# The output product of a two-layer graph kernel: from a two by two by two to a two by three by three scheme

## The chip, the cores and the metric

The kernel runs on one core of one Trainium2 chip. The metric is the device time of one execution in microseconds; before the change it is 2888.91 us, the median of three runs (2888.81 to 2894.07).

## What is computed

Two layers over 128 graphs of 64 nodes with 768 features, all in float32. Cut to what matters:

```python
def _L1_gnn_ref(seq_inputs, Wq, bq, Wk, bk, Wv, bv, Wf, bf, graph_mask):
    q = _heads(seq_inputs @ Wq + bq)          # 6 heads of 128
    k = _heads(seq_inputs @ Wk + bk)
    v = _heads(seq_inputs @ Wv + bv)
    scores = jnp.einsum('bhqd,bhkd->bhqk', q, k) / np.sqrt(HEAD_SIZE)
    probs = jax.nn.softmax(scores + bias, axis=-1)
    ctx = jnp.einsum('bhqk,bhkd->bhqd', probs, v)
    ctx = ctx.transpose(0, 2, 1, 3).reshape(...)
    return ctx @ Wf + bf

x = _layernorm(x + _L0_gnn_ref(x, adj, ...))  # tanh attention of 12 heads, elu, gate
x = _layernorm(x + _L1_gnn_ref(x, ..., adj))
```

The change concerns the last product, `ctx @ Wf + bf`, with the residual `x +` around it.

## The kernel before

The 8192 rows (tokens) are 64 tiles of 128 rows; two tiles make a pair, four a quad. Phase A runs over the 32 pairs and computes layer 0 and layer 1's values v; phase B runs over the 16 quads and computes queries, keys, attention and the output. Every large product of 768 by 768 is made by a scheme of seven products instead of eight (`TURNS`): tokens, inner features and output features are each split in two, seven sums of blocks of the tokens meet seven sums of blocks of the matrix, and the seven results are added up in a certain way. A weight matrix therefore lies in SBUF as seven blocks of 384 by 384 (`places`). The sums for the first layer's matrices are made in place; those of wq, wk and wf are made on GpSimd during phase A by `to_there`, which loads small pieces into a free part of `zone`, sums them and stores seven blocks to DRAM, and `matrix` loads them back later.

The order of the work on each engine is written out. A class `Beat` keeps a clock whose unit is one product: `beat.product` emits the matmuls of one product and puts the read of its result 1.5 beats later; `beat.start` steps a generator whose yields are waits in beats; `tick` emits what has become due. This fixes the order in which instructions stand in each engine's queue. The engines then run through their queues freely, waiting only on semaphores.

Phase B, for a quad q and f = 0, 1, 2 (each f is a pair of heads):

- `queries` and `keys` (both `by_feature`, matmuls on L417): seven products of three matmuls of 256 columns. Results stand in three PSUM sums. P1 is copied by ACT (L397) or biased (L400), P6 and P5 are read by VectorE into `q_u`/`k_u` (L393), P7 by L403, P3 by L409, P4 by L406. P7 and P4 stand in the same PSUM sum, so P4's matmuls wait for P7's read.
- `slab`: the attention of one f. Scores `s_ps` (L936), mask and maximum on VectorE (L946, L950), L952, the exponential on ACT, sum, reciprocal, L961, then a copy on ACT (L975), a transposing DMA (L976), two copies (L980), the product with v `c_ps` (L992), two copies (L1006), two transposing DMAs (L1007) and four copies into `cT` (L1014). Its steps stand beats apart and interleave with the products. For the very last f the transposes are made on TensorE (L970, L990).
- for the quad before, at f = 1 the first output (i = 0) and at f = 2 the second (i = 1), each of a pair of tiles: `operands` makes the four sums of tokens on VectorE (L290, tile `sc`, a single buffer) during `keys`; `rows_of` loads the pair's rows of layer 0 (`y`, L1034) and adds the bias on GpSimd (L1039); `output` follows the keys with `by_token` (L321): seven products of three matmuls of 384 columns in three PSUM sums. P1 is copied by ACT (L1058), VectorE reads the others (L1063 to L1082), GpSimd adds rows to three of the parts (L1052). `normed` then takes the statistics on VectorE, the power on GpSimd (L345, L346), scales on ACT (L1093) and stores the rows (L1095).

All DMAs stand in SP's queue, in the order in which they were emitted; a DMA that waits holds the ones behind it. PSUM has five buffers (`dense_b`) for sums in phase B. The bias of the values goes through wf into `bf_sb` once, by `last_bias` (L898), between queries and keys of q = 1, f = 0.

Of the kernel before, what the change touches and what calls it, by code (L numbers as in the profile page):

```python
# [27 lines left out]
F32 = mybir.dt.float32  # L31
# [3 lines left out]
ALU = mybir.AluOpType  # L35
# [4 lines left out]
P = 128  # L40
N = 64
D = 768
KC = D // P
KH = KC // 2
HALF = D // 2
H0, E0 = 12, 64
H1, E1 = 6, 128
BANK = 512
# [8 lines left out]
W11, W21, W22, T1, T2, T3, N4 = range(7)  # L57
# [13 lines left out]
    ("P4", 1, X22, N4),  # L71
)

# [53 lines left out]
class Beat:  # L127
# [31 lines left out]
    def tick(self):  # L159
        while self.events and self.events[0][0] < self.now + 1:  # L160
            heapq.heappop(self.events)[-1]()
        self.now += 1

    def until(self, there):
        while not there():
# [8 lines left out]
def two_layers(  # L174
# [21 lines left out]
    nc = tc.nc  # L196
# [19 lines left out]
    bv_sb = const.tile([P, KC], F32, name="bv_sb")  # L216
# [3 lines left out]

    places = [const.tile([P, 7, KH, HALF], F32, name=f"w_{i}") for i in range(3)]
    place = {"w0": 0, "h_w": 1, "wv": 2, "wq": 0, "wk": 1, "wf": 2}
# [18 lines left out]
        engine.tensor_tensor(t[:, N4], t[:, W21], t[:, T2], ALU.subtract)  # L241


    w_there = {n: dram.tile([P, 7, KH, HALF], F32, name=f"{n}_there") for n in ("wq", "wk", "wf")}

    def to_there(w, name):
        blocks = w.rearrange("(k c p) (m q n) -> k m c q p n", k=2, p=P, m=2, n=P)
# [49 lines left out]
    def sums_of_tokens(engine, s, b11, b12, b21, b22):  # L297

        if engine is nc.vector:
            plus(s[:, 0], b21, b22)  # L300
            plus(s[:, 1], s[:, 0], b11, ALU.subtract)
            yield 1
            plus(s[:, 2], b11, b21, ALU.subtract)
            plus(s[:, 3], b12, s[:, 1], ALU.subtract)
        else:
            engine.tensor_tensor(s[:, 0], b21, b22, ALU.add)
            engine.tensor_tensor(s[:, 1], s[:, 0], b11, ALU.subtract)
            yield 1
            engine.tensor_tensor(s[:, 2], b11, b21, ALU.subtract)
            engine.tensor_tensor(s[:, 3], b12, s[:, 1], ALU.subtract)  # L310

    def by_token(name, blocks, w, reads):

        sums = [sb(dense[0], [P, BANK], "dense", f"{name}{i}") for i in range(3)]
        begun = set()
        for what, to, xb, wb in TURNS:
            ps = sums[to][:, 0:HALF]

            def emit():
                for c in range(KH):  # L320
                    nc.tensor.matmul(  # L321
                        ps,
                        lhsT=blocks[xb][:, c, :],
                        rhs=w[:, wb, c, :],
                        start=(c == 0 and to not in begun),
                        stop=(c == KH - 1),
                        skip_group_check=True,
                    )
# [35 lines left out]
    ready, dense = {}, []  # L364
# [69 lines left out]
    def phase_a(pa, ps_a, dst_pool):  # L434
# [400 lines left out]
        for p in range(n_pairs):  # L835
            ta, tb = tiles_of(p)
            A = {"t": ta, "p": p, "side": 0}
# [38 lines left out]
    blocks = {}  # L876
# [9 lines left out]


    def phase_b(pb, ps_b):
        beat.start(matrix("wf", 1), 2)
        bf_sb = row(bf, "bf_sb", pb)  # L890

        def last_bias():

            for m, parts in enumerate((((0, W11), (1, W21)), ((0, W11), (0, T1), (1, W22)))):
                ps = sb(dense[0], [P, BANK], "dense", f"bias_ps_{m}")[:, 0:HALF]
                steps = [(k * KH + c, wb, c) for k, wb in parts for c in range(KH)]
                for i, (at, wb, c) in enumerate(steps):
                    nc.tensor.matmul(  # L898
                        ps,
                        lhsT=bv_sb[:, at : at + 1].to_broadcast([P, P]),  # L900
                        rhs=ready["wf_sb"][:, wb, c, :],
                        start=(i == 0),
                        stop=(i == len(steps) - 1),
                    )
                to = bf_sb[:, m * HALF : (m + 1) * HALF]
                nc.vector.tensor_tensor(to, to, ps, ALU.add)

        def part(name):
            return sb(pb, [P, HALF], "part", name, 7)

        def load(Q):

# [106 lines left out]
        def operands(Q, i):  # L1019

            while not Q.get("done"):
                yield 1
            q, c = Q["q"], Q["c"][i]
            s = sb(pb, [P, 4, KH, P], "sc", f"sc_{q}_{i}", 1)
            b = [c[:, 0, :, 0], c[:, 1, :, 0], c[:, 0, :, 1], c[:, 1, :, 1]]
            yield from sums_of_tokens(nc.vector, s, *b)
            Q["ob", i] = b + [s[:, k] for k in range(4)]

        def rows_of(Q, i):
            q = Q["q"]  # L1030
# [9 lines left out]
                yield 1  # L1040

        def output(Q, i):
            q = Q["q"]
            ya, yb = Q["y", i, 0], Q["y", i, 1]
            lo, hi = slice(0, HALF), slice(HALF, D)
            u = {}
            name = f"o_{q}_{i}_"

            def with_rows(k, of, y, m):
                def work():  # L1050
                    u[k] = part(f"{name}{k}")
                    nc.gpsimd.tensor_tensor(u[k], u[of], y[:, m], ALU.add)  # L1052

                beat.soon(work)

            def p1(ps):
                u[1] = part(f"{name}1")
                nc.scalar.copy(u[1], ps)  # L1058
                with_rows(4, 1, yb, lo)

            def p6(ps):
                u[2] = part(f"{name}2")
                nc.vector.tensor_tensor(u[2], u[1], ps, ALU.add)  # L1063
                with_rows(5, 2, ya, hi)

            def p2(ps):
                nc.vector.tensor_tensor(ya[:, lo], ya[:, lo], ps, ALU.add)

            def p5(ps):
                u[3] = part(f"{name}3")  # L1070
                nc.vector.tensor_tensor(u[3], u[1], ps, ALU.add)
                with_rows(6, 3, yb, hi)

            def p7(ps):
                nc.vector.tensor_tensor(yb[:, hi], u[6], ps, ALU.add)

            def p4(ps):
                nc.vector.tensor_tensor(yb[:, lo], u[4], ps, ALU.add)
                beat.start(normed(yb, 4 * q + 2 + i), 0)

            def p3(ps):
                nc.vector.tensor_tensor(ya[:, hi], u[5], ps, ALU.add)  # L1082
                beat.start(normed(ya, 4 * q + i), 0)

            by_token(name, Q["ob", i], ready["wf_sb"], dict(P1=p1, P2=p2, P3=p3, P4=p4, P5=p5, P6=p6, P7=p7))
# [18 lines left out]
        for q in range(n_quads + 1):  # L1104
            for f in range(3):
                if q < n_quads and (q or f):
                    queries(q, f, blocks, part)
                if q == 1 and f == 0:
                    last_bias()
# [72 lines left out]
```

## Time and profile before

The profiled execution took 2889.98 us, of which the span from first to last instruction is 2888.1; the granted clock of TensorE was 0.992 on average.

| | us |
|---|---|
| median of three runs | 2888.91 |
| profiled execution, its span | 2889.98, 2888.1 |
| phase A, up to the first queries of phase B | 1455.7 |
| TensorE busy from 1500 to 2800 us | 1300.0 of 1300 |
| VectorE busy from 2000 to 2500 us | 227 of 500 |
| GpSimd busy from 2000 to 2500 us | 96 of 500 |
| output product L321 (`o`), 1344 records | 471.3 |
| bias product L898, 30 records | 9.8 |
| GpSimd's row additions L1039, 64 of 1.81 | 114.8 |
| GpSimd's additions L1052, 96 of 1.12 | 107.3 |

How to read it: PE is TensorE, PEld its weight loads, DVE is VectorE, POOL is GpSimd, SPq is SP issuing DMAs. A group such as `o<-w,sc` is named by what it writes and reads. Busy time of PE overlaps: a record of 256 columns lasts 0.38 us in the table, but the next one starts 0.22 later.

### The profile page before, as it was taken

The page shows a single profiled execution, that of the slowest core. Times are in us where ns is not written, and L with a number is a line of the kernel's source. Part 1 is how long each engine was busy: PE and PEld are TensorE (multiplying, and loading weights), DVE is VectorE, ACT ScalarE, POOL GpSimd, SP SyncE. Part 2 cuts the span into 40 slices and gives each one's busy share as a digit, 9 for nine tenths or more (in the row PEclk, how much of TensorE's full clock was granted, in tenths as well). Part 3 has the DMA queues.
Part 4 walks back from the last instruction along what each step waited for, and adds up shares of the span by engine and source line. Part 5 has one row for each costly group of instructions (what it writes and reads, how often), then busy time and mean ns, then how long its engine had stood idle before and what let it go on. Part 6 is the DMA issues. An engine that isn't in the chain of part 4 may idle for free.

```text
span 2888.1 us, 42411 instructions
## 1 busy us (share of the span) xinstructions
PE 2825.2 (98%) x15586; PEld 1927.7 (67%) x15586; DVE 1851.1 (64%) x3555; ACT 1324.3 (46%) x1594; POOL 1182.0 (41%) x1106
## 2 busy tenths in 40 slices
PE   7899999999999999999799999999999999999998
PEld 4455555555555555555577777777777787877775
DVE  6887888888888988888534444444444444444444
ACT  2655555655556655665423333333333343333332
POOL 5666767767666656665201111221212211112113
PEclk9999999999999999999899999999999999999999
DMA  6677777778776666667864354443544434544432
GB/s 203 152 181 210 192 189 210 197 193 206 187 195 170 177 166 175 177 164 200 231 172 109 95 121 118 110 121 81 123 120 124 103 99 106 130 123 103 110 94 79
DMA packets 670350, 434.29 MB, mean 150 GB/s; under 512 B 442816, under 2 KB 616384, under 8 KB 670144
## 3 DMA queue, kind: packets, MB, share of 16 engines
q1 hardware_dynamic: 670144, 431.59, 58.0%
q8 instruction: 123, 2.02, 0.3%
q14 instruction: 83, 0.68, 0.1%
HBM read 199.07 MB, written 132.32 MB: 115 GB/s over the span
## 4 chain that ended last, share of the span: by engine, by line
PE 90%; DVE 3%; DMA 3%; ACT 1%; issue 0%; SPq 0%; POOL 0%; POOLq 0%; DVEq 0%; ACTq 0%
PE o L321 15%; PE k L417 15%; PE q L417 15%; PE v L321 14%; PE h L321 13%; PE g L321 12%; PE f_all L723 2%; PE s_ps L936 2%; PE c_ps L992 2%; DMA th_d<-bc_e 1%; ACT bc_e L714 0%; PE bias_ps L898 0%; DMA elu_turned<-xg_parts 0%; DVE mix L748 0%; DVE mix L753 0%
## 5 line engine op out<-in xcount | busy, mean ns | idle before, releaser
L321 PE MATMUL h<-w,zone 128*128 128x384 f32 x1320 | 448.4, 495 | 22.6 <-ACT h L514 12.4
L417 PE MATMUL q<-zone,w 128*128 128x256 f32 x2016 | 452.1, 382 | 6.9 <-issue 4.0
L417 PE MATMUL k<-zone,w 128*128 128x256 f32 x2016 | 446.2, 381 | 0.9 <-ACT k_u L397 0.9
L321 PE MATMUL g<-w,zone 128*128 128x384 f32 x1320 | 442.2, 490 | 4.8 <-DVE gate L568 3.7
L417 PEld LDWEIGHTS q<-zone,w 128*128 128x128 f32 x2016 | 382.5, 191 | 68.6 <-issue 6.2
L417 PEld LDWEIGHTS k<-zone,w 128*128 128x128 f32 x2016 | 380.6, 190 | 57.0 <-issue 5.0
L1039 POOL TENSOR_TENSOR y<-y,bf_sb 128x768 f32<-128x768 f32 x64 | 114.8, 1813 | 741.7 <-DMA y<-x_there 638.5
L321 PEld LDWEIGHTS h<-w,zone 128*128 128x128 f32 x1320 | 250.9, 192 | 196.5 <-ACT h L514 13.6
L321 PEld LDWEIGHTS g<-w,zone 128*128 128x128 f32 x1320 | 248.2, 190 | 177.5 <-DVE gate L568 12.7
L321 PE MATMUL o<-w,sc 128*128 128x384 f32 x768 | 268.0, 493 | 2.8 <-DVE sc L290 2.8
L345 POOL TENSOR_TENSOR rs<-rs,power 128x1 f32<-128x1 f32 x128 | 71.1, 556 | 460.6 <-DVE rs L343 460.6
L321 PE MATMUL v<-w,x_sums 128*128 128x384 f32 x768 | 258.5, 486 | 0.9 <-DVE x_sums L290 0.9
L643 POOL TENSOR_TENSOR bc_e<-th_d,w_dst_sb 128x768 f32<-128x768 f32 x64 | 119.8, 1873 | 237.9 <-ACT th_d L538 210.4
L321 PEld LDWEIGHTS v<-w,x_sums 128*128 128x128 f32 x768 | 145.7, 190 | 103.1 <-DVE x_sums L290 2.1
L321 PEld LDWEIGHTS o<-w,sc 128*128 128x128 f32 x768 | 144.1, 191 | 100.0 <-DVE sc L290 3.8
L321 PE MATMUL o<-w,cT 128*128 128x384 f32 x576 | 203.3, 489 | 0.5 <-ACT cT L1002 0.5
L1052 POOL TENSOR_TENSOR o<-o,y 128x384 f32<-128x384 f32 x96 | 107.3, 1119 | 183.4 <-issue 82.7
L1006 ACT COPY parts<-c_ps 128x1024 uint16<-128x1024 uint16 x94 | 95.4, 1015 | 150.1 <-PE c_ps L992 150.1
L321 PEld LDWEIGHTS o<-w,cT 128*128 128x128 f32 x576 | 107.9, 190 | 72.5 <-issue 2.6
L714 ACT COPY bc_e<-th_d 128x1536 uint16<-128x1536 uint16 x64 | 123.4, 1928 | 42.3 <-DMA th_d<-bc_e 42.0
L638 POOL TENSOR_SCALAR zone<-zone 128x768 f32<-128x768 f32 x64 | 137.4, 2147 | 0.0
L639 POOL TENSOR_TENSOR xg_parts<-xg_parts,zone 128x768 f32<-128x768 f32 x64 | 122.3, 1910 | 23.7 <-POOL zone L638 9.8
(163 smaller groups left out, 4448.2 us busy)
## 6 DMA issues: line engine op xcount, KB each, us to landing
zone<-ops_there SPq DMA_DIRECT2D x224, 192.0 KB, 4.6
zone<-in_xT SPq DMA_DIRECT2D x32, 768.0 KB, 6.5
zone<-in_x SPq DMA_DIRECT2D x64, 384.0 KB, 4.0
bc_e<-there SPq DMA_DIRECT2D x128, 192.0 KB, 3.4
x_there<-mix SPq DMA_DIRECT2D x64, 384.0 KB, 4.2
ops_there<-x_sums SPq DMA_DIRECT2D x32, 768.0 KB, 3.3
v_there<-v SPq DMA_DIRECT2D x128, 192.0 KB, 2.6
v<-v_there SPq DMA_DIRECT2D x128, 192.0 KB, 3.9
```

Source lines behind the costliest of these rows:

```text
L321: nc.tensor.matmul(ps, lhsT=blocks[xb][:, c, :], rhs=w[:, wb, c, :], start=(c == 0 and to not in begun), stop=(c == KH - 1), skip_group_ch ...
L345: nc.gpsimd.tensor_tensor(rs[:, 0:1], rs[:, 0:1], power, ALU.pow)
L417: nc.tensor.matmul(ps, lhsT=w[:, wb, c, f * P : (f + 1) * P], rhs=blocks[xb][:, c, :], start=(c == 0 and to not in begun), stop=(c == KH - 1),
L638: nc.gpsimd.tensor_scalar(xs, xs, 1.0, None, ALU.add)
L639: nc.gpsimd.tensor_tensor(xg, xg, xs, ALU.mult)
L643: nc.gpsimd.tensor_tensor(bc, th, w_dst_sb, ALU.mult)
L714: nc.scalar.copy(halves(e), by_halves(d))
L723: nc.tensor.matmul(f_all[b * N : (b + 1) * N, at : at + E0 + 1], lhsT=e[rows, hd // 2 * P + b * N : hd // 2 * P + (b + 1) * N], rhs=(h[row ...
L936: nc.tensor.matmul(s_ps[b * N : (b + 1) * N, i, r, :], lhsT=qT[:, r, at], rhs=kT[:, r, at], start=True, stop=True,)
L1006: nc.scalar.copy(by_halves(parts), halves(c_ps[:, r].rearrange("p i t -> p (i t)")))
L1039: nc.gpsimd.tensor_tensor(y, y, bf_sb, ALU.add)
L1052: nc.gpsimd.tensor_tensor(u[k], u[of], y[:, m], ALU.add)
```

## The change

The output product is made by another scheme: the tokens are split in two, the inner features in three (parts of 256), the output features in three (parts of 256, `THIRD`), and 15 products take the place of 18. Each product is two matmuls of 256 columns instead of three of 384.

- `FIFTEEN` lists the products: the PSUM sum it stands in, the tokens' operand, the matrix's block and the parts of the rows that its result is added to or taken from. Six PSUM sums are used; a sum goes on from product to product, and VectorE reads what it holds after each product and adds it to, or takes it from, a third of the rows `y` in place (16 reads of 128 by 256). The ACT copy and GpSimd's three additions go.
- `operands` makes eleven sums of 128 by 256 on VectorE, two to a step, instead of four of 128 by 384.
- `wf` isn't prepared in phase A any more. At the start of phase B nine loads bring it in as nine blocks, `last_bias` is made from these (18 matmuls of 256 columns), and then GpSimd makes 15 sums of 128 by 512 in place.
- A product of the output counts 2/3 of a beat (`length`), so the output is 10 beats long instead of 7, and what stands beside it keeps its place in beats. `part` has 5 buffers of 256 instead of 7 of 384.

```diff
-    def product(self, emit, then):
+    def product(self, emit, then, length=1):
         emit()
-        self.at(self.now + 1.5, then)
-        self.tick()
+        self.at(self.now + 1.5 * length, then)
+        self.tick(length)
...
+FIFTEEN = (
+    (0, "3", 9, ((-1, 1),)),
+    (2, "A2", 6, ((1, 0),)),
+    (1, "12", 0, ((-1, 3),)),
+    (0, "11", 7, ((1, 4),)),
+    (3, "A5", 3, ((1, 3),)),
+    (1, "A3", 1, ((1, 4),)),
+    (0, "2", 11, ((-1, 3),)),
+    (4, "14", 2, ((1, 2),)),
+    (1, "7", 4, ((-1, 1),)),
+    (0, "10", 12, ((1, 5),)),
+    (4, "5", 14, ((1, 1),)),
+    (1, "A1", 5, ((-1, 2),)),
+    (0, "1", 8, ((1, 0), (-1, 2))),
+    (5, "6", 13, ((-1, 4),)),
+    (1, "0", 10, ((1, 5),)),
+)
...
-            for name, w in (("wq", wq), ("wk", wk), ("wf", wf)):
+            for name, w in (("wq", wq), ("wk", wk)):
                 yield from to_there(w, name)
...
-        beat.start(matrix("wf", 1), 2)
+        def last_matrix():
+            blocks = wf.rearrange("(c k p) (m n) -> k m p c n", k=3, p=P, m=3)
+            for k in range(3):
+                for m in range(3):
+                    nc.sync.dma_start(wf_sb[:, 3 * k + m], blocks[k, m])
+                    yield 1
+            yield 4
+            for m in range(3):
+                last_bias(m)
+                yield 1
+            for to, a, b, op in (
...
+            ):
+                nc.gpsimd.tensor_tensor(wf_sb[:, to], wf_sb[:, a], wf_sb[:, b], op)
+                yield 2
+        beat.start(last_matrix(), 2)
...
+            s = sb(pb, [P, 11, 2, P], "sc", f"sc_{Q['q']}_{i}", 1)
...
+            for k, (name, sign, a, b, op) in enumerate(sums):
+                of[name] = s[:, k]
+                nc.vector.scalar_tensor_tensor(s[:, k], of[a], sign, of[b], ALU.mult, op)
+                if k % 2:
+                    yield 1
...
+            for at, xb, wb, to in FIFTEEN:
+                begun = at in sums
+                if not begun:
+                    sums[at] = sb(dense[0], [P, BANK], "dense", f"o_{q}_{i}_{at}")[:, 0:THIRD]
+                ps = sums[at]
+                def emit():
+                    for c in range(2):
+                        nc.tensor.matmul(ps, lhsT=of[xb][:, c, :], rhs=wf_sb[:, wb, c, :], ...)
+                def read(ps=ps, to=to):
+                    for sign, b in to:
+                        k, n = divmod(b, 3)
+                        part_of = y[k][:, n * THIRD : (n + 1) * THIRD]
+                        nc.vector.tensor_tensor(part_of, part_of, ps, ALU.add if sign > 0 else ALU.subtract)
+                        left[k] -= 1
+                        if not left[k]:
+                            beat.start(normed(y[k], 4 * q + 2 * k + i), 0)
+                beat.product(emit, read, 2 / 3)
```

In the changed program's SP queue, both transposing DMAs of `c_ps` of f = 1 (L1007 before) stand ahead of the loads of `y` for the second output; before, one of them stood behind those loads. `c_ps` itself stands after four of the seven products of the query that follows an output; before, it stood after all seven.

More of the change, by code (lines that the diff above doesn't have):

```diff
@@ L45 @@
 HALF = D // 2
+THIRD = D // 3
 H0, E0 = 12, 64
@@ L152, in start, with tick @@
         self.at(time, lambda: step(time), order)
-    def product(self, emit, then):
+    def product(self, emit, then, length=1):
         emit()
-        self.at(self.now + 1.5, then)
-        self.tick()
-    def tick(self):
-        while self.events and self.events[0][0] < self.now + 1:
+        self.at(self.now + 1.5 * length, then)
+        self.tick(length)
+    def tick(self, length=1):
+        while self.events and self.events[0][0] < self.now + length:
             heapq.heappop(self.events)[-1]()
-        self.now += 1
+        self.now += length
     def until(self, there):
@@ L241, in sums_of_weights @@
         engine.tensor_tensor(t[:, N4], t[:, W21], t[:, T2], ALU.subtract)
-    w_there = {n: dram.tile([P, 7, KH, HALF], F32, name=f"{n}_there") for n in ("wq", "wk", "wf")}
+    w_there = {n: dram.tile([P, 7, KH, HALF], F32, name=f"{n}_there") for n in ("wq", "wk")}
     def to_there(w, name):
@@ L888, in phase_b @@
     def phase_b(pb, ps_b):
-        beat.start(matrix("wf", 1), 2)
         bf_sb = row(bf, "bf_sb", pb)
[L892 to L906, printed above, removed]
+        wf_sb = places[place["wf"]].rearrange("p a b c -> p (a b c)")[:, 0 : 15 * 2 * THIRD]
@@ new lines, in phase_b @@
+        wf_sb = wf_sb.rearrange("p (a c n) -> p a c n", a=15, c=2)
+        def last_matrix():
[9 more added lines that the diff above has]
+            for to, a, b, op in (
+                (9, 0, 7, ALU.add),
+                (10, 5, 8, ALU.add),
+                (11, 3, 7, ALU.subtract),
+                (12, 3, 8, ALU.subtract),
+                (13, 4, 7, ALU.add),
+                (14, 1, 2, ALU.subtract),
+                (1, 1, 4, ALU.add),
+                (1, 1, 9, ALU.add),
+                (4, 14, 13, ALU.add),
+                (14, 14, 7, ALU.add),
+                (5, 5, 3, ALU.add),
+                (5, 4, 5, ALU.subtract),
+                (3, 3, 6, ALU.add),
+                (6, 6, 0, ALU.add),
+                (6, 6, 8, ALU.add),
+            ):
+                nc.gpsimd.tensor_tensor(wf_sb[:, to], wf_sb[:, a], wf_sb[:, b], op)
+                yield 2
@@ new lines, in last_bias @@
+        def last_bias(m):
+            ps = sb(dense[0], [P, BANK], "dense", f"bias_ps_{m}")[:, 0:THIRD]
+            for i in range(H1):
+                k, c = i % 3, i // 3
+                nc.tensor.matmul(
+                    ps,
+                    lhsT=bv_sb[:, i : i + 1].to_broadcast([P, P]),
+                    rhs=wf_sb[:, 3 * k + m, c, :],
+                    start=(i == 0),
+                    stop=(i == H1 - 1),
+                )
+            to = bf_sb[:, m * THIRD : (m + 1) * THIRD]
+            nc.vector.tensor_tensor(to, to, ps, ALU.add)
@@ L908, in part @@
+        beat.start(last_matrix(), 2)
         def part(name):
-            return sb(pb, [P, HALF], "part", name, 7)
+            return sb(pb, [P, 2 * P], "part", name, 5)
         def load(Q):
@@ L1022, in operands @@
                 yield 1
[L1023 to L1027, printed above, removed]
+            c = Q["c"][i]
+            A = [c[:, :, k, m] for m in range(2) for k in range(3)]
+            s = sb(pb, [P, 11, 2, P], "sc", f"sc_{Q['q']}_{i}", 1)
+            of = {f"A{k}": a for k, a in enumerate(A)}
+            sums = (
+                ("3", 1.0, "A0", "A2", ALU.subtract),
+                ("12", -1.0, "3", "A3", ALU.subtract),
+                ("2", 1.0, "A5", "A4", ALU.subtract),
+                ("11", 1.0, "2", "3", ALU.subtract),
+                ("14", 1.0, "A0", "A3", ALU.add),
+                ("7", -1.0, "A1", "A3", ALU.subtract),
+                ("0", 1.0, "A1", "A4", ALU.add),
+                ("10", 1.0, "0", "A5", ALU.subtract),
+                ("5", 1.0, "A0", "A1", ALU.subtract),
+                ("1", 1.0, "10", "A2", ALU.subtract),
+                ("6", 1.0, "A3", "A4", ALU.subtract),
+            )
+            for k, (name, sign, a, b, op) in enumerate(sums):
[3 more added lines that the diff above has]
+                    yield 1
+            Q["ob", i] = of
         def rows_of(Q, i):
@@ L1042, in output @@
         def output(Q, i):
[L1043 to L1085, printed above, removed]
+            q, of = Q["q"], Q["ob", i]
+            y = [Q["y", i, k] for k in range(2)]
@@ new lines, in output @@
+            sums = {}
+            left = [sum(b // 3 == k for *_, to in FIFTEEN for _, b in to) for k in range(2)]
+            for at, xb, wb, to in FIFTEEN:
[5 more added lines that the diff above has]
+                    for c in range(2):
+                        nc.tensor.matmul(
+                            ps,
+                            lhsT=of[xb][:, c, :],
+                            rhs=wf_sb[:, wb, c, :],
+                            start=(c == 0 and not begun),
+                            stop=(c == 1),
+                            skip_group_check=True,
+                        )
+                def read(ps=ps, to=to):
[7 more added lines that the diff above has]
+                beat.product(emit, read, 2 / 3)
@@ L1107, in phase_b @@
                     queries(q, f, blocks, part)
-                if q == 1 and f == 0:
-                    last_bias()
                 if before and at_place(q, f) is not None:
```

## The prediction

> **What bounds the kernel now.** I read the busy shares first, then the chain of waits in order of time over one steady stretch, then the timeline of the same stretch, and last the timeline of the kernel's end. The page's first lines:
>
> ```profile
> span 2888.1 us, 42411 instructions
> PE 2825.2 (98%) x15586; PEld 1927.7 (67%) x15586; DVE 1851.1 (64%) x3555; ACT 1324.3 (46%) x1594; POOL 1182.0 (41%) x1106
> ```
>
> TensorE is busy nearly always; VectorE at 64% is an average of a full first phase and a half empty second one. The change lies in the second phase (from 1456 us), so the chain there decides (start, length, what, number of pieces):
>
> ```profile
> 1628.32 9.06 PE k L417 x42
> 1637.39 1.03 PE c_ps L992 x32
> 1638.42 4.07 PE o L321 x12
> 1642.49 1.08 PE s_ps L936 x32
> 1643.57 9.87 PE o L321 x30
> 1653.44 9.06 PE q L417 x42
> 1662.51 1.03 PE c_ps L992 x32
> 1663.54 9.26 PE k L417 x42
> ```
>
> There is nothing but TensorE, and the pieces add up to the period of about 89 us for a quad: every microsecond put into or taken out of this row moves the end. A matrix instruction stands as two records: one output is 21 matmuls and 42 records. The next two fences are timelines (start, length, engine, line, what, idle before): the key product ahead of an output with f = 2, and the last quad's end.
>
> ```profile
> 1664.64 1.24 SPq L1007 DMA_TRANSPOSE s<-parts  x1
> 1665.94 1.05 SPq L1034 DMA_DIRECT2D y<-x_there  x2
> 1667.66 0.42 DVE L393 TENSOR_TENSOR k_u<-k_u,k 128x256 f32<-128x256 f32 x1 [0.80 <-PE k L417]
> 1669.28 3.57 POOL L1039 TENSOR_TENSOR y<-y,bf_sb 128x768 f32<-128x768 f32 x2 [12.31 <-DMA y<-x_there]
> 1670.25 0.48 DVE L403 SCALAR_TENSOR_TENSOR zone<-k,bk_sb,k_u 128x256 f32<-128x256 f32 x1 [2.17 <-PE k L417]
> ```
>
> ```profile
> 2848.26 3.57 POOL L1039 TENSOR_TENSOR y<-y,bf_sb 128x768 f32<-128x768 f32 x2
> 2850.48 1.76 DVE L290 SCALAR_TENSOR_TENSOR sc<-cT 128x384 f32<-128x384 f32 x1
> 2851.91 1.19 POOL L1052 TENSOR_TENSOR o<-o,y 128x384 f32<-128x384 f32 x1
> 2852.28 1.23 DVE L290 SCALAR_TENSOR_TENSOR sc<-sc,cT 128x384 f32<-128x384 f32 x1
> 2853.44 0.54 DVE L290 SCALAR_TENSOR_TENSOR sc<-cT 128x384 f32<-128x384 f32 x1
> ```
>
> The second one is what I build on. An operand sum of L290 takes 0.55 us (median). Started while GpSimd's row addition of L1039 runs (it ends at 2851.83), it takes 1.76 and ends 0.41 after it; the next, beside L1052, takes 1.23. So a VectorE sum whose two inputs both lie in SBUF waits out a GpSimd addition. The reads with one input in PSUM do not: L403 above takes 0.48 inside L1039. In the steady stretches the four sums run from 0.5 us before the key product's start to 2.1 after it, the row additions start 5.6 to 6.9 after it: they never meet.
>
> **The change part by part.**
>
> *TensorE's work.* Records 256 wide: the q product of 42 takes 9.06, so 0.2157 each (the 9.26 of a product behind c_ps or s_ps has 0.2 for the entry, which stays). Records 384 wide: 9.87 less 0.2 over 30, and 3.87 over 12, give 0.3223. Old output 42 x 0.3223 = 13.54, new 60 x 0.2157 = 12.94: 0.60 less. 29 outputs lie before the end stretch: -17.3 us. Bounds: nothing less than that by count of columns, and up to +0.4 an output (+12) if the reads below stall it.
>
> [...]
>
> *Reads.* Old: six of 0.555 (VectorE), one ACT copy, three GpSimd additions. New: 16 of 128x256 from PSUM, each like L393's 0.42. Sums in a PSUM bank are continued two products later, so a read has 2 x 0.863 = 1.73 us. Set out on VectorE with the slab's five operations (0.68 to 0.69 each, 0.20 for the reciprocal), with 0.27 from a product's end to its read (P6 of k ends at 2.59, its read starts at 2.86): the reads come through, the tightest (behind the pair of L946 and L950) with about 0.7 us in hand. I take nothing. The slab's c_ps comes four products into the next q instead of at its end: the last of the slab's five ends 10.8 us after the output's start, the copy of L975 (1.05), the transposing DMA (3.1 to landing), then in ACT's order the normalised row (1.03), q_u (0.37) and two copies (1.38): ready at 18.8, needed at 19.4. Covered too, narrowly.
>
> *Operand sums.* Four of 384 become eleven of 256. From L290's 0.55 and 128 columns less at the slope of 384 to 512 (0.13): 0.42 each, and starts 0.34 apart, 0.45 where one needs the one before. Their order in the key product is: four, k_u of P6, two, k_u of P5, four, P7's read, one, then P3's and P4's reads. With k at 0: the first four 0.65 to 2.3, P6's read at 2.86, two until 4.0, P5's read 4.08 to 4.50, the next four 4.43 to 6.0, P7's read at 6.7. P4 goes into P7's bank at 7.76 and waits for that read.
>
> *f = 1 (the first output of a quad).* GpSimd's row additions start 5.56 to 6.36 after k (trace), and the load's place in SP's queue doesn't change. The fourth of the last group starts at 5.6: a few may meet. Price if it does: 0.9. Bounds 0 and 16 x 0.9; I take 1.5 us in all.
>
> *f = 2 (the second output).* Here a move further up pulls something. SP's queue held, ahead of the y loads, only the first transpose of c_ps. With c_ps earlier, both transposes stand ahead, and both are done earlier: c_ps ends at 20.4 from the first output's start, ACT's two copies (1.01 each) at 21.7 and 22.7, the transposes (1.24 each on SP) until 24.2, the loads at 24.25; the output lasts 12.94 + 1.28 for s_ps = 14.22, so k begins at 14.22 + 9.06 + 1.23 = 24.5. The loads go out at k - 0.25 instead of k + 2.46, and the row additions (3.3 to 3.7 later, trace) start at k + 3.1 to 3.5: in the middle of the sums. Two additions of 1.81: one sum gets in ahead, one between, so sum five ends at 5.9, P5's read at 6.2, the second addition at 7.7, the four sums at 9.2, P7's read at 9.65. P4 starts at about 9.8, not 7.76: 2.0 us, 2.25 if the first addition comes ahead of sum four, 2.4 if it comes a microsecond later. Below nothing isn't possible, nothing if it starts after 5.6. TensorE has nothing else queued ahead of P4, so all of it is on the chain; ACT and SP don't wait for it. I take 2.1 x 15 (quads 1 to 15) = +31.5; bounds 0 and 36.
>
> *The end, from 2829.80.* The old stretch lasts 58.3. New: c_ps ends at 16.75 (18.15 before, as the transposes fit into the products). Sum one at 18.7; then BN statistics stand ahead of the other sums, and GpSimd's two additions (from 21.7) alternate with them: the first read, behind all eleven sums, ends at 28.5, and the fourth product (same bank) waits for it, 7 us idle. Twelve products of 0.863: 39.0. The next sums wait for the single sc buffer (+2.0), then the same again: idle 7 us, end of products at 61.0, and 8.4 for reads, statistics, normalising and the store (7.3 before). 69.4 - 58.3 = +11. Without the two collisions +4. I take +11.
>
> *The matrix.* Bias: 15 matmuls of 384 (9.7) against 18 of 256 (7.8): -1.9. The nine loads go out behind v's (1463 to 1472), land by some 1477 at w<-wf's 3.8, are needed at 1480; not hidden, they cost up to 5. The 15 sums on GpSimd (some 1.26 each between L1052's 0.99 and L1039's 1.81) take 19 us after that, done 30 us ahead of the first output. Removed from phase A: 36 small loads, 9 stores, 36 GpSimd sums between 645 and 895 us. There TensorE waited 4.6 us by the view of waits (3.8 for bc_e, 0.8 for zone L307, which the chain leads back to the load zone<-in_wf), and from 900 to 1340 hardly at all: -4, bounds 0 and -5.
>
> Sum: -17.3 + 1.5 + 31.5 + 11 - 1.9 - 4 = +20.8. The profiled execution took 2889.98 (span 2888.1 and 1.9 around it), 1.07 over the median of 2888.91: 2910.8 on its scale, 2909.7 against the median. I say 2910.
>
> **The rivals.** *The collision in k doesn't come* (the loads stay after k + 2.1, or VectorE's sums get through). For it: in the steady stretches before there is not one such meeting; against: SP's order, and the two long sums at the end. Then 2910 - 31.5 - 1.5 - 7 = 2870, faster. *Only half of it* (the loads about at k + 2, one sum caught): +1 an output, 2893. *VectorE also falls behind inside the output*: 16 x 0.42, 3.6 for the slab and 1.5 for one row's statistics are 11.8 us of work in 14.2, and a read later than 1.73 us stops TensorE; at 0.6 an output 29 x 0.6 = 17 more, 2928; it decides from 0.7 us of lateness on. That the products aren't saved at all (256 wide records dearer than q's) I hold for very unlikely: the shapes are q's own.
>
> **How the numbers follow.** Collision as worked out 0.53 (its own range 2900 to 2920), none 0.20 (2866 to 2882), half 0.12 (2885 to 2900), more stalls 0.15 (2918 to 2940). The range for 8 in 10 runs from 2872 to 2927: it leaves out some 0.12 below and 0.08 above. 0.2% is 5.8 us, about what a measurement of this kernel tells from no change: faster (under 2883) 0.22, within 0.07, slower 0.71.
>
> **What would show it.** Right: y loads on SP at or before k's start where f = 2; sums of 1.7 to 2.2 us there; TensorE's k idle some 2 us ahead of its last three matmuls, waiting for VectorE; the chain showing output pieces of about 13.2; GpSimd's L1039 counterpart 3.5 us after k. Wrong: k at 9.1 there (then 2870), waits inside the output, or waits for c_ps (ACT's copies).

## The result and the profile after

The changed kernel takes 2900.18 us (median of 8 runs, 2898.62 to 2902.55), the kernel before 2889.72 in the same session (8 runs, 2887.45 to 2894.07). The ratio is 1.0034, with a 95% interval of 1.0023 to 1.0045: slower by 10.5 us. The forecast was slower by 20.8. The direction and the mechanism held, its size did not.

The first lines of the page after:

```profile
span 2899.4 us, 43977 instructions
PE 2810.6 (97%) x16168; PEld 2039.8 (70%) x16168; DVE 2059.3 (71%) x4100; ACT 1305.7 (45%) x1562; POOL 1081.5 (37%) x989
```

The span has grown by 11.3 us, and TensorE's busy time has fallen by 14.6: the products are cheaper, as meant, and TensorE now waits. The chain of waits, in order of time, over a second output and the key product ahead of it (start, length, what, number of pieces):

```profile
1656.06 2.60 PE k L452 x12
...
1659.17 2.29 DVE sc L1112 x2
1661.46 0.33 DVE k_u L428
1661.79 1.63 DVE sc L1112
...
1663.45 1.09 DVE sc L1112 x3
1664.54 0.41 DVE zone L438
...
1664.99 1.56 PE k L452 x6
1666.56 2.59 PE o L1143 x12
...
1670.23 10.56 PE o L1143 x48
```

Before, this stretch of the chain held TensorE alone. Now the key product is cut: 36 of its 42 records come in time, and the last six (P4) start 8.93 us after the product's start instead of 7.76, behind operand sums (L1112) and P7's read (L438). From 1656.06 to 1666.56 it lasts 10.50 us; undisturbed it takes 9.06 (before it stood at 9.26, with 0.2 for the entry behind c_ps, which now lies in the query). The output behind it shows the gain: 2.59 + 10.56 = 13.15 us where the second outputs before had 3.87 + 9.87 = 13.74. The timeline of the same product (start, length, engine, line, what, idle before) says what the sums waited for:

```profile
1654.41 1.27 SPq L1077 DMA_TRANSPOSE sT<-parts  x1
1655.73 1.06 SPq L1122 DMA_DIRECT2D y<-x_there  x2
1659.09 2.37 DVE L1112 SCALAR_TENSOR_TENSOR sc<-cT 128x256 f32<-128x256 f32 x2
1659.25 3.88 POOL L1127 TENSOR_TENSOR y<-y,bf_sb 128x768 f32<-128x768 f32 x2 [10.03 <-DMA y<-x_there]
1661.72 1.70 DVE L1112 SCALAR_TENSOR_TENSOR sc<-cT 128x256 f32<-128x256 f32 x1
1664.46 0.48 DVE L438 SCALAR_TENSOR_TENSOR zone<-k,bk_sb,k_u 128x256 f32<-128x256 f32 x1
```

Both transposes of c_ps are done before the key product starts, the rows' loads go out 0.33 us ahead of it, and GpSimd's two additions run from 3.2 to 7.1 us after it. The sums that meet them take 1.70, and 2.37 for a pair, instead of 0.42 each; the long one of the pair and the one of 1.70 each end 0.3 us behind an addition's end. The view of waits from 1560 to 2830 us (engine and line, whom it waited for: us in all, times, longest) has one entry for TensorE:

```profile
PE k L452 <- DVE zone L438: 17.9, 15, 1.7
```

It is 1.19 us on average in the 15 second outputs; with 0.27 for starting again (six records in 1.56 instead of 1.29) it makes the 1.46 that these key products have grown by on average.

At the end of the kernel, the timeline shows two long idles of TensorE, and something the prediction didn't have:

```profile
2854.37 2.07 PE L1143 MATMUL o<-w,sc 128*128 128x256 f32 x4 [4.03 <-DVE y L1156]
2856.24 3.53 PE L1143 MATMUL o<-w,cT 128*128 128x256 f32 x8
2859.61 4.48 PE L1143 MATMUL o<-w,sc 128*128 128x256 f32 x20
2878.15 2.08 PE L1143 MATMUL o<-w,sc 128*128 128x256 f32 x4 [6.22 <-DVE y L1156]
```

Behind the idle, 12 records take 5.24 us (2854.37 to 2859.61); the next 20 go at 0.216 each, at which 12 would take 2.59. The view by windows gives the granted clock (window, length, busy us and instructions of TensorE, weight loads, VectorE, ScalarE and GpSimd, then clock, DMA share, GB/s):

```profile
2854.37:2859.60 5.23, 5.23 (x12) 4.21 (x13) 1.45 (x4) 0.00 (x0) 0.00 (x0) 0.50 0.13 50
2859.60:2864.00 4.40, 4.40 (x22) 3.88 (x21) 2.10 (x5) 0.00 (x0) 0.00 (x0) 1.00 0.00 0
```

The granted clock is 0.50 behind the idle of 4.03 us, and 1.00 again 5.2 us later.

### The profile page after: what moved, and what is told of

It reads as the page before. It is cut to its first block, busy times and chain, and to the rows that moved or that the text cites. A ratio compares the mean times of both kernels' runs of the same rounds, so it can differ in the third digit from the quotient of the medians.

```text
span 2899.4 us, 43977 instructions
## 1 busy us (share of the span) xinstructions
PE 2810.6 (97%) x16168; PEld 2039.8 (70%) x16168; DVE 2059.3 (71%) x4100; ACT 1305.7 (45%) x1562; POOL 1081.5 (37%) x989
## 4 chain that ended last, share of the span: by engine, by line
PE 88%; DVE 6%; DMA 2%; ACT 1%; issue 0%; SPq 0%; POOL 0%; DVEq 0%; POOLq 0%; ACTq 0%
PE q L452 15%; PE o L1143 14%; PE v L356 14%; PE h L356 14%; PE g L356 13%; PE k L452 13%; DVE sc L1112 3%; PE f_all L758 2%; PE s_ps L1006 2%; PE c_ps L1062 2%; DMA th_d<-bc_e 0%; DMA elu_turned<-xg_parts 0%; DMA w<-wk_there 0%; DVE k_u L428 0%; PE bias_ps L966 0%
## 5 line engine op out<-in xcount | busy, mean ns | idle before, releaser
L452 PE MATMUL q<-zone,w 128*128 128x256 f32 x2016 | 460.5, 384 | 6.3 <-DMA zone<-ops_there 4.3
L452 PE MATMUL k<-zone,w 128*128 128x256 f32 x2016 | 447.2, 380 | 18.8 <-DVE zone L438 17.9
L1127 POOL TENSOR_TENSOR y<-y,bf_sb 128x768 f32<-128x768 f32 x64 | 122.6, 1935 | 650.2 <-DMA y<-x_there 604.8
L1143 PE MATMUL o<-w,sc 128*128 128x256 f32 x1408 | 337.9, 385 | 13.5 <-DVE y L1156 10.2
L1143 PEld LDWEIGHTS o<-w,sc 128*128 128x128 f32 x1408 | 265.3, 191 | 54.0 <-DVE y L1156 11.1
L1156 DVE TENSOR_TENSOR y<-y,o 128x256 f32<-128x256 f32 x512 | 206.7, 415 | 132.9 <-PE o L1143 127.3
L1024 ACT ACTIVATE s<-s 128x512 f32<-128x512 f32 x48 | 30.1, 626 | 251.1 <-DVE s L1022 251.1
L1169 ACT ACTIVATE y<-y,rs 128x768 f32<-128x768 f32 x64 | 65.6, 1025 | 165.1 <-POOL rs L381 165.0
L1112 DVE SCALAR_TENSOR_TENSOR sc<-cT 128x256 f32<-128x256 f32 x224 | 135.1, 615 | 0.1
```

The costliest lines, as they stand in the source:

```text
L452: nc.tensor.matmul(ps, lhsT=w[:, wb, c, f * P : (f + 1) * P], rhs=blocks[xb][:, c, :], start=(c == 0 and to not in begun), stop=(c == KH - 1),
L1112: nc.vector.scalar_tensor_tensor(s[:, k], of[a], sign, of[b], ALU.mult, op)
L1127: nc.gpsimd.tensor_tensor(y, y, bf_sb, ALU.add)
L1143: nc.tensor.matmul(ps, lhsT=of[xb][:, c, :], rhs=wf_sb[:, wb, c, :], start=(c == 0 and not begun), stop=(c == 1), skip_group_check=True,)
L1156: nc.vector.tensor_tensor(part_of, part_of, ps, ALU.add if sign > 0 else ALU.subtract)
```

## Where the time went

By the starts of the same products in the two profiled executions, against the terms of the prediction:

| stretch or term | predicted | measured |
|---|---|---|
| first phase (second phase starts 1451.38, before 1455.67) | -4 | -4.3 |
| bias product, 7.77 for 9.7 | -1.9 | -1.9 |
| 29 outputs, 0.59 each | -17.3 | -17.1 |
| key products of first outputs (9.15, unchanged) | +1.5 | 0 |
| key products of second outputs, 15 | +31.5 | +22.0 |
| what is left between 1451 and 2827 | 0 | -1.2 |
| end, from the next to last quad's second output (72.1, before 58.3) | +11 | +13.8 |
| sum | +20.8 | +11.3 |

## The experiments

Each time is a median; the kernel before had 2889.49, 2889.09 and 2889.36 us in the three sessions, so that the values stand beside each other and beside 2900.18.

**e1: the additions in the q product.** The second output's rows are started one product earlier.

```diff
+                if before and at_place(q, f) == 1:
+                    beat.start(rows_of(before, 1))
                 if q < n_quads and (q or f):
                     queries(q, f, blocks, part)
...
                     beat.start(operands(before, i))
-                    beat.start(rows_of(before, i))
+                    if i == 0:
+                        beat.start(rows_of(before, i))
```

> The changed kernel, with the row loads and GpSimd's row additions of a quad's second output started ahead of the q product instead of the key product. Theory (VectorE's operand sums wait out GpSimd's additions, and P7's read comes late behind them): the additions now run in the q product, where VectorE only reads PSUM; the 15 key products of 10.4 to 11.1 us come back to about 9.1, that is 15 x 1.46 = 22 us less: 2878 us. Rival (eleven sums instead of four are too many for VectorE ahead of P7's read, whatever GpSimd does): those key products stay at 10.4 or more, 2900 us. Second rival (the row loads' traffic, which now runs beside the transposes and v's loads, takes the gain back elsewhere): 2885 to 2900, with new waits for c_ps or v.

2877.90 us, ratio to the kernel before 0.9956 (0.9941 to 0.9971). By the windows view from 1560 to 2800 us, first the changed kernel, then e1:

```profile
1560.00:2800.00 1240.00, 1223.34 (x7852) 1051.45 (x7851) 731.20 (x1699) 428.14 (x637) 147.43 (x165) 1.00 0.45 112
```

```profile
1560.00:2800.00 1240.00, 1240.00 (x7945) 1070.38 (x7944) 709.98 (x1739) 437.34 (x651) 144.18 (x168) 1.00 0.45 113
```

TensorE's 16.7 us of idle are gone to nothing, with more VectorE instructions (1739 for 1699) in less busy time. The ten sums that stand ahead of P7's read now fit there (the eleventh stands behind it); the view of waits has no entry left in this stretch, so no second wait took the place of the first.

**e2: the additions later.** `beat.start(rows_of(before, i), 2 * i)`.

> The changed kernel, with the row loads of a quad's second output issued two products later, about where they were in the kernel before. Theory: the additions start some 6 to 7 us after the key product's start, after the tenth sum; the key products come back to about 9.1 (22 us less, 2878), and the output's first read of the rows may wait a little for them (0 to 0.5 us an output, up to 2886). Rival (the count of sums alone): 2900. If the loads go out only one product later than now, the additions meet other sums and the loss is between 0 and 22 us.

2879.49 us, 0.9962 (0.9947 to 0.9977). In its timeline the loads go out 3.7 us after the key product's start (1654.3) and the additions start 9.4 after it, later than expected, behind all the sums:

```profile
1663.74 3.58 POOL L1127 TENSOR_TENSOR y<-y,bf_sb 128x768 f32<-128x768 f32 x2 [16.08 <-DMA y<-x_there]
```

The output's first reads stand behind them and still come through. TensorE waits once more, for 1.7 us, in the last quad. Both sides of the sums are free: the loss belongs to the place between.

**e3: no additions.** Additions and loads moved together in e1 and e2; here the loads stay and the additions go. The rows of 15 second outputs leave without bf.

```diff
-                nc.gpsimd.tensor_tensor(y, y, bf_sb, ALU.add)
+                if i == 0 or q + 1 == n_quads:
+                    nc.gpsimd.tensor_tensor(y, y, bf_sb, ALU.add)
```

> The changed kernel without the additions of the bias to the rows of the second outputs of quads 0 to 14 (those rows leave without bf); the loads stay where they are. It tells the additions from the loads, which move together in the other variants. Theory: without GpSimd's instructions no sum takes over 0.5 us in the key product, k is about 9.1 and the time 2878. Rival (the loads' writes into SBUF hold VectorE up): 2900, with sums of 1.5 us and more left. Rival (the count of sums): 2900, with sums of 0.42.

2877.84 us, 0.9957 (0.9943 to 0.9972); TensorE is busy for all of the 1240 us, and the sums ahead of second outputs take 0.42, with the loads where they were: the loads' writes cost nothing that shows here.

**e4: the first phase's part back.** `wf` again in the lists of `w_there` and `matrices()`.

> The changed kernel, with the preparation of wf put back into the first phase (loads, GpSimd sums and stores of its parts; their result is no longer read). Theory: it costs what its removal gave, the second phase starts 4.3 us later (at 1455.7 instead of 1451.4) and the time is 2904.5. Rival (the 4.3 us came from somewhere else, such as the order of the first phase's queues at its end): the second phase starts at 1451.4, 2900.

2904.86 us, 1.0049 (1.0032 to 1.0065), 4.7 more than the changed kernel. The view of waits from 600 to 920 us has its two entries of before again, 4.3 us in all (none in the changed kernel); the larger:

```profile
PE f_all L758 <- ACT bc_e L749: 3.5, 2, 2.7
```

The second phase starts at 1457.6, 6.2 us behind the changed kernel's 1451.4 and later than the 1455.7 expected. Of the 6.2, the two waits are 4.3. Behind the wait of 2.7, the 48 records of `f_all` take 1.58 us and the next 30 of `g` 10.59, where they take 0.93 (behind another wait) and 9.87 elsewhere in e4: 1.4 us more. The kernel before has the same there, 1.58 and 10.65, with a granted clock of 0.50 from 806.0 to 809.4; the changed kernel's stays at 1.00. A wait of 1.65 us at 1444.9, which the kernel before lacks, stands in the changed kernel too (at 1438.8), so it isn't part of this cost. Of the 6.2 the middle gave back 0.4 and the end 1.2. That the preparation costs some 4 to 6 us is shown; that the 1.4 are the clock's is taken over from the kernel before.

**e5: the same additions in thirds.**

```diff
-                nc.gpsimd.tensor_tensor(y, y, bf_sb, ALU.add)
+                for m in range(3):
+                    at = slice(m * THIRD, (m + 1) * THIRD)
+                    nc.gpsimd.tensor_tensor(y[:, at], y[:, at], bf_sb[:, at], ALU.add)
```

> The changed kernel, with each of GpSimd's row additions (128x768, about 1.8 us) cut into three of 128x256; loads and places in the queues stay, so that the additions still meet the sums, with as much data. Theory (a VectorE sum waits for the end of the GpSimd instruction that is running): sums in the key product take at most about 1.1 us instead of 1.5 to 2.4, five or six of them get in between the six additions instead of one or two, and P7's read ends by about 7.5 to 8.2 us; k of a second output is 9.1 to 9.6, the time 2878 to 2886. Rival (both engines share a bandwidth, so that what counts is the data that GpSimd moves meanwhile): k stays at 10.4 or more, 2900 us.

2883.00 us, 0.9975 (0.9965 to 0.9984). One such key product in the timeline:

```profile
1657.61 5.06 POOL L1129 TENSOR_TENSOR y<-y,bf_sb 128x256 f32<-128x256 f32 x6 [9.81 <-DMA y<-x_there]
1661.14 0.94 DVE L1112 SCALAR_TENSOR_TENSOR sc<-cT 128x256 f32<-128x256 f32 x1
```

The same data pass through GpSimd and meet the same sums, but no sum takes over 0.98 us (2.08 with whole additions), and by the view of waits of the same stretch (1560 to 2830) TensorE's fall from 17.9 us in 15 products to 5.7 in 10. The longest sum is 1.1 us shorter, as much as one instruction of GpSimd is on average (5.06 / 6 = 0.84 us for 3.88 / 2 = 1.94), while the data are the same: in these two runs a sum's delay went with the length of the instruction that it met, not with the data. GpSimd pays in turn: 5.06 us where the two whole additions took 3.88. How much of that is sums in between, and how much the starting of six instructions for two, isn't shown.

**t1: the end's rows earlier.** The last quad's rows are started in the output before each.

```diff
                     beat.until(lambda: ("ob", i) in before)
+                    if (q, f) in ((n_quads - 1, 2), (n_quads, 1)):
+                        beat.start(rows_of(quads[n_quads - 1], q + 1 - n_quads), 2)
                     output(before, i)
```

(with `rows_of` left out of its old place there)

> The changed kernel, with the rows of the last quad's two outputs loaded and added during the output before each, instead of behind the sums. Only the end changes (72.1 us from the start of the next to last quad's second output's product to the end of the span). Theory: the sums there no longer meet GpSimd's additions; two meetings of 3.0 us each go, TensorE's idles of 4.0 and 6.2 us become about 1.0 and 3.2, the end stretch 66, the time 2894; if the half granted clock after each idle goes with the idle's length, up to 5 us more, 2889. Rival (the single sc buffer and the statistics ahead of the sums set those idles): 2900.

2896.38 us, 1.0024 (1.0014 to 1.0035), 3.8 less than the changed kernel. The end stretch fell by 7.5 (64.6 us from 2829.35), the idle of 4.03 went (1.0 was expected to stay) and that of 6.22 became 3.02 (3.2 was expected); but 2 us came back in the key product ahead of it, where TensorE waits 3.2 instead of 1.25 (t3 shows why).

**t3: sums in a buffer of their own, started early.**

```diff
+            if Q["q"] == n_quads - 1 and i == 1:
+                s = places[place["wq"]].rearrange(...)
+            else:
                 s = sb(pb, [P, 11, 2, P], "sc", f"sc_{Q['q']}_{i}", 1)
...
                 nc.vector.scalar_tensor_tensor(s[:, k], of[a], sign, of[b], ALU.mult, op)
+                if Q["q"] == n_quads - 1 and k == 1:
+                    Q["ob", i] = of
...
+                    if (q, f) == (n_quads, 1):
+                        beat.start(operands(before, 1), 1)
```

> The changed kernel, with t1's edit, the last output's sums in a buffer of their own (the place of wq, which is free by then) and started during the output before, and each of the last two outputs started behind the first two sums instead of all eleven. Theory: TensorE is idle in the end only for about 1.7 us ahead of the first sum; from there two outputs of 12.95 and 8.0 behind them: 18.5 + 25.9 + 8.0 = 52.4 us instead of 72.1, the time 2880.5 (2 to 3 us more if the clock is halved after that idle too). Rival (VectorE cannot carry sums, reads and statistics of two outputs at once, and the reads hold TensorE up): 60 us or more, 2888.

2893.67 us, 1.0017 (1.0008 to 1.0027), 6.5 less instead of 20: a miss. The reason stands in the timeline of the last quad's key product:

```profile
2818.82 7.64 POOL L1133 TENSOR_TENSOR y<-y,bf_sb 128x768 f32<-128x768 f32 x4 [10.70 <-DMA y<-x_there]
2827.20 2.92 PE L452 MATMUL k<-zone,w 128*128 128x256 f32 x6 [4.47 <-DVE zone L438]
```

The additions written for the output ran in the key product, four in a row: GpSimd had nothing ahead of them, and took them up as soon as their rows had landed. The sums between take 1.7 to 2.0 us each, and P4 there waits 4.47. The other two additions met the early sums inside the next output, where TensorE waits 4.5 us in all for reads; two of these waits are 1.61 us each, and the 12 records behind the second take 5.28 us (2862.23 to 2867.51) where full speed gives 2.59. In this run a place in the program held GpSimd only by what stood ahead of it in GpSimd's own queue.

**c1: e1 and t3 together.**

> The changed kernel with e1's edit (rows of the second outputs in the q product) and the whole end of t3. If both losses are what this study says and don't overlap: 2900 - 22 - 20 = 2858 us, that is 31 under the kernel before, of which the terms are -17 (outputs), -2 (bias), -4 (no preparation of wf in the first phase), -6 to -8 (end). Rival (a part of the gain comes back as another wait): 2866 or more.

2870.33 us, 0.9932 (0.9920 to 0.9945). Faster than both kernels, 12 us short of the expectation: 1.1 us of waits left in that key product, and 4.5 for reads in the end, the longest 3.2 where sums meet the additions. The rival's condition (2866 or more) came true.

**c2: the two meetings taken apart.** A GpSimd addition of 128x1 that reads the scores holds the last first output's row additions until these are multiplied; the last sums start eight beats later.

```diff
-            yield 2
+            yield 5 if behind else 2
+            if behind:
+                s = behind()
+                g = tiny.tile([P, 1], F32, tag="gate", name=f"gate_{q}_{i}")
+                nc.gpsimd.tensor_tensor(g, s[:, 0, 0, 0:1], s[:, 0, 0, 1:2], ALU.add)
...
-                        beat.start(operands(before, 1), 1)
+                        beat.start(operands(before, 1), 8)
```

> c1, with the two meetings that were left in its end taken apart: the row additions of the last quad's first output wait (by a tiny GpSimd addition that reads the scores) until the scores are multiplied, in the middle of the output before, and the last output's sums start eight products later, behind the other additions. Theory (GpSimd took up additions as soon as their rows had landed, wherever they stood in the program, and met sums in the key product and in the output): the key product's 1.1, the output's 3.2 and 0.8 us of waits go, 2870 becomes 2863 to 2866. Rival (VectorE has too much to do there anyhow): 2869 or more.

2865.86 us, 0.9909 (0.9893 to 0.9924), within the range expected. The key product's wait and the 3.2 are gone; a read 2.2 us late is left.

**t4: TensorE kept busy.** On the changed kernel, to tell the idle from the clock.

```diff
+        def fill(count, name):
+            ps = sb(ps_b, [P, 4, 2, N], "s", name, 1).rearrange("p i r j -> p (i r j)")[:, 0:THIRD]
+            for _ in range(count):
+                nc.tensor.matmul(ps, lhsT=ident, rhs=wf_sb[:, 0, 0, :], start=True, stop=True)
...
                 beat.product(emit, read, 2 / 3)
+                if q + 1 == n_quads and xb == "12":
+                    fill((9, 14)[i], f"fill_{i}")
```

> The changed kernel, with products into an unused bank, whose result nobody reads, put between the third and the fourth product of the last two outputs: 9 and 14 matmuls (3.9 and 6.0 us at 0.2157 a record) into idles of 4.0 and 6.2 us. Nothing comes earlier by them. Theory (the granted clock falls to a half because TensorE was idle): the 12 records behind each idle take 2.6 us instead of 5.2, the time is 5 us less, 2895. Rival (the slow records have another cause, such as the operands just written, or the clock falls at these moments whatever TensorE does): 2900, or up to 6 more where the added products themselves run at the half clock and last longer than the idle.

2894.89 us, 1.0017 (1.0008 to 1.0026), 5.3 less, for work that nobody uses:

```profile
2848.62 4.05 PE L1001 MATMUL fill<-w,ident 128*128 128x256 f32 x18
2854.50 1.13 PE L1148 MATMUL o<-w,sc 128*128 128x256 f32 x4 [1.84 <-DVE y L1161]
2855.47 1.89 PE L1148 MATMUL o<-w,cT 128*128 128x256 f32 x8
```

P4 starts at the same distance from the stretch's start as in the changed kernel (27.1 us); its 12 records take 2.70 instead of 5.24, and by the windows view the granted clock is 1.00 from 2854 to 2859, where the changed kernel has 0.50 (2854.37 to 2859.60). So the half clock came from the idle.

**c3: c2 with four such matmuls** behind the last c_ps, in 1.7 us of idle.

> c2, with four matmuls into an unused bank (1.7 us) in the 1.7 us in which TensorE waits for the first sum of the last quad. Theory (an idle of 1.7 us can halve the clock for some 3.5 us behind it): 0 to 2 us less than c2, depending on how often c2's profile shows the half clock there. Rival: the same as c2, or up to 1 us more where the four don't fit.

2863.87 us, 0.9908 (0.9895 to 0.9922). The median is 2.0 under c2's, but the ratios, 0.9908 and 0.9909, are the same within their intervals, so a gain over c2 isn't shown. By median it is the lowest of all: 25 us under the kernel before, 36 under the changed one.

## Why the prediction was right, and where it was wrong

*Right, to a few tenths:* the products' price (0.59 for 0.60 an output, and no read stops TensorE inside an output ahead of the end) and the bias. The chain was right too: the transposes, then the loads ahead of the key product (0.3 us for the 0.25 given), additions at 3.1 to 3.5 in twelve of the fifteen products (3.9 to 4.7 in three), sums that wait them out, P7's read, P4. e1, e2 and e3 each take away one link and win back 21 to 22 us. The first phase's 4.3 for 4 is in part luck: the 4.6 us of waits went, and with them a granted clock of 0.50 from 806.0 to 809.4, 1.4 us by the records behind it, which the working didn't have; a new wait of 1.65 us at 1438.8 took about as much back.

*The step that failed* is the size of the second outputs' term: "Two additions of 1.81: one sum gets in ahead, one between, so sum five ends at 5.9, P5's read at 6.2, the second addition at 7.7, the four sums at 9.2, P7's read at 9.65", priced at 2.1 us. Measured is 1.46 on average (1.3 to 2.0). The sums wait out the additions as said, but the second addition doesn't start as late as 5.9. It starts as soon as the first has ended, at 5.1 in seven of the fifteen products (the one shown is one of them), and ends at 7.1, not 7.7. The pair takes 3.83 to 3.94 there, some 0.3 more than the 3.57 it took before, where the working has 0.6 to 1.0 around and between the two (7.7 less 3.62 and a start at 3.1 to 3.5). In the other eight the second addition ends at 7.4 to 8.5, but VectorE gets on meanwhile, and at most two sums are left behind it, not four. P7's read ends at about 8.9 on average instead of 9.65, and TensorE waits 1.19 us, with 0.27 for starting again. Fifteen times 0.64 is 9.5 us, as much as the whole difference between forecast and result; the other terms' errors (first outputs, end, rest) cancel.

*First outputs:* 1.5 us were put in, none came; there the additions meet the eleventh sum at most, which stands behind P7's read, and TensorE doesn't wait for it.

*The end:* 13.8 for 11, by two errors that nearly cancel. The idles are 13.5 us in all (1.73, 4.03, 1.53 and 6.22), below the 2 + 7 + 2 + 7 of the working. But the working gave the products behind them their full speed. Behind the idles of 1.73, 4.03 and 6.22 us, 8, 12 and 12 records took 3.52, 5.24 and 5.29 us where full speed gives 1.73, 2.59 and 2.59: 7.1 us more. The kernel before shows the same in its timeline:

```profile
2853.57 5.83 PE L321 MATMUL o<-w,sc 128*128 128x384 f32 x12 [2.76 <-DVE sc L290]
2859.24 2.10 PE L321 MATMUL o<-w,cT 128*128 128x384 f32 x6
```

Twelve records take 5.67 us there, to the next one's start at 2859.24, and 3.87 in the steady stretch; the granted clock is 0.50 from 2853.99 to 2857.40.

*The rivals:* no collision (2870) is what e1 and e3 built, at 2878, where only the steady stretches are free and the end still collides. *Only half of it* (2893, loads at about k + 2) didn't come either: the loads go out 0.3 us ahead of the key product, and the price of a meeting lies between that rival's 1 us and the 2.1 taken. VectorE falling behind inside an output didn't come either: ahead of the end no read in an output holds TensorE up.

## What to carry to other kernels

When a transfer moves forward, follow the work that its landing releases: in t3 nothing in the program text held GpSimd back once its queue was empty, and in the changed kernel the harm was done by a GpSimd addition that started eight microseconds before its result was read (1659.25 to 1667.51 in the product shown). Where VectorE instructions such as the operand sums here (two SBUF inputs, 0.42 us alone and up to 2.08 beside a GpSimd addition of 1.8 to 2.0) sit ahead of a read that TensorE waits for, keep such additions out of that stretch (e1: 22 us less), or cut them short (e5: 17 less). When summing up idles of TensorE, add the slow products behind them (7.1 us for idles of 13.5 here).

## What the runs showed of the hardware that was not expected

In the last 110 us of the 13 profiles (the two kernels and the eleven variants) an idle of 2.76 us and more was followed by slow records in all 16 cases, such as the 12 in 5.24 us for 2.59; one of 2.51 (e5) was not. After 1.73 us, at the same place of 11 kernels, they came in six and not in five; after 1.53 in none of eight. In the two kernels' profiles the windows view gives a granted clock of 0.50 there: before, for 3.41 us from 2853.99, behind the idle of 2.76; in the changed kernel for 3.41 us from 2845.90, behind 1.73, and for 6.83 us from 2852.73 and from 2876.62, where the idles of 4.03 and 6.22 end. But near 242 us, in the first phase, they have idles of 2.80 (before) and 2.85 us (after), and the clock stays at 1.00.

So in these two profiles the length of one idle doesn't settle it. From 90 us on, the granted clock changes at nine moments before (such as 805.99, 809.40, 1406.74, 2853.99, 2857.40) and at eleven after (such as 1402.06, 2845.90, 2849.32, 2852.73, 2859.55), and those of one profile all lie whole multiples of 3.413 us apart. Cut at these moments, from 100 us on, into pieces of 3.413 us, the two have eight pieces at full clock with 2.12 us or more without a matmul record (two of them behind the last product), and each is followed by a half clock. Of the 1608 with less, one is: it holds the idle of 1.73 us, and beside it 1.58 us of `c_ps`'s small matmuls. One with 1.75 us, in a key product (from 2019.88), isn't. The 2.80 us near 242 are cut into 1.86 and 0.94, the 2.85 into 1.59 and 1.25; the 2.76 at the end lie in one piece. That an idle halves the clock or not by where it falls fits these two profiles; no run moved an idle to test it.
